# Four decoder layers on one core: the second layer's probabilities turned by a DMA, the pieces of the row maxima in one transpose

## The chip, the cores and the metric

The kernel runs on one core of a Trainium2 chip. A core has five engines that run side by side, each with its own queue of instructions: TensorE (PE, matrix products; PEld is its loading of weights), VectorE (DVE), ScalarE (ACT), GpSimd (POOL) and SyncE (SP, which issues all DMAs here). Matrix products land in PSUM, which only PE writes and only DVE and ACT read; everything else lives in SBUF (the "arena") or in DRAM. The metric is the device time of one execution in microseconds (us), the median of several runs. The profile is of one execution more.

## The reference, cut to what matters

Four decoder layers follow each other on x of shape (16, 128, 256), each with 16 heads of 16. The second layer (L1) has two attentions with quantised operands; the third and fourth have two plain attentions each.

```python
def _fq(x, delta, zp, n_bits):                      # second layer
    xi = round(x / delta) + zp
    xq = jnp.clip(xi, 0.0, 2.0 ** n_bits - 1.0)
    return (xq - zp) * delta
...
sim = jnp.einsum('bhid,bhjd->bhij', _fq(q, dq, 128.0, 8), _fq(k, dk, 128.0, 8)) * SCALE
attn = jax.nn.softmax(sim, axis=-1)
out = jnp.einsum('bhij,bhjd->bhid', _fq(attn, dw, 0.0, 8), _fq(v, dv, 128.0, 8))
...
logits = jnp.einsum('bhqd,bhkd->bhqk', qh, kh) / jnp.sqrt(depth)      # third and fourth layer
attn = jax.nn.softmax(logits + mask, axis=-1)
out = jnp.einsum('bhqk,bhkd->bhqd', attn, vh)
```

The quantised probabilities are whole numbers from 0 to 255 times a step `dw`.

## The kernel before

**Groups and the order.** The batch of 16 is cut into 8 groups of 2 (`GB = 2`, `NG = 8`). Each group runs the whole chain of layers; groups don't depend on each other. The program first makes a list of steps (`plan.step`): a step has one or more ways (an engine, a price in us that its author wrote down, the function that issues the instructions), what it reads and what it writes. `Plan.order` then lays out all steps of all groups as a list scheduler would: it takes the step that can begin first by those prices, and among steps that can begin at the same time the one with the lowest `level` plus `LEADS[group][stage]`. `LEADS` is a table of 8 x 20 numbers, so it sets which group goes first where. Memory comes from the arena by the same pass. The instructions are then issued in that order, once, in straight line: each engine works its own list in order, and waits on semaphores for the others. So an instruction that has to wait holds up all that stand behind it on its engine.

**PE has three tilings.** "full" (128 x 128, projections, feed-forward and transposes), "rows" (four matmuls of 32 rows side by side, the scores), "cols" (four of 32 columns side by side, the products of probabilities and values).

**Second layer** (`quantized_attention`, `attention`). For one batch element `j` and half `c` of its heads (8 heads), in order: the scores on PE into the one `ps` block of PSUM; the row maxima (DVE, L1099); their subtraction (DVE, L1112); the exponential (ACT, L1118); the sums and their reciprocals times 1/dw (DVE, L1124 to L1127); the division into shares, head by head, with a magic constant that rounds to whole numbers (POOL, `share`, L1133); the bound at 255 and the cast to bf16 (DVE, L1137, block `eb`). `attention` turns `eb`, queries first, into `eT`, keys first: eight PE transposes into a PSUM block `pt` (L905) and a copy to SBUF (ACT L910 or DVE L911). When both halves are there, `out_of` issues `products` (PE, L879, 16 matmuls) into `po`, and ACT scales it by `dwv` (L1143). A step of the kind occurs 8 groups x 2 attentions x 2 elements x 2 halves = 64 times, the products 32 times.

**Third and fourth layer** (`plain_attention`, `batch`). Here the scores are computed twice: once queries first, to get the row maxima of 16 heads (DVE, L1236 or L1251), and once keys first, so that the exponentials come out already turned. The maxima must be subtracted in the second form, and this is done on PE: `split` cuts each maximum into three bf16 pieces that add up to it (block `mq`, four 128-column planes, one for each of four heads of a strip of 32 rows), four PE transposes (L1271) and a copy of 128 x 512 (ACT, L1275) turn them into `mt`, and `below` adds them to the scores by four matmuls with a matrix `three` of ones in three of 32 rows (L844, 512 columns each). The fp32 products of keys and queries follow (L833). This is done 64 times. Then come the exponential (ACT, L1302), the products with values and with ones (PE, L879, fp32) and the division (DVE, L1314, L1315).

**Weights.** `weight` loads a 256 x 256 block by a DMA on SP (L634); a block that is still in the arena is not loaded again. All DMAs stand in the one queue of SP. Feed-forward and projections are `features_first` (L675) and `tokens_first` (L688), fp32.

Of the kernel before, what the change touches and what calls it, by code (L numbers as in the profile page):

```python
# [8 lines left out]
F32 = mybir.dt.float32  # L9
BF16 = mybir.dt.bfloat16  # L10
# [6 lines left out]
P = 128  # L17
# [49 lines left out]
SLOTS = {"sm": (64, 46), "row": (128, 12), "pw": (2048, 4), "ps": (8192, 1), "mq": (1024, 4)}  # L67
# [8 lines left out]
    [83, 27, 167, 130, 306, 193, 74, 226, 213, -45, 163, -53, 159, -84, 116, -64, 214, 400, 286, 283],  # L76
    [-69, -856, -114, -260, -60, 57, -165, -14, -2, -22, -386, -90, 144, -71, -260, -59, -586, -159, -213, -106],
    [49, -47, -11, 314, -162, 407, 51, 168, -361, -27, -172, 141, -4, -107, 36, 5, -54, 235, 78, 92],
    [-16, -228, 250, -173, -19, 106, 36, 203, -176, 14, 164, 2, 299, -144, 10, 309, -45, 154, 150, -1],
    [210, 166, 422, 222, 201, 790, 324, 499, 569, 334, 435, 116, 502, 205, 259, 760, 536, 716, 652, 178],  # L80
    [330, 158, 210, 147, 392, 517, 262, 488, 490, 57, 292, 77, 380, 208, 348, 38, 542, 447, 523, 1141],
    [267, 148, 130, 158, 333, 376, 220, 605, 204, -29, 43, 216, 340, 164, 196, 435, 324, 999, 754, 951],
    [288, 156, 593, 320, 407, 313, 255, 389, 233, 323, -30, 86, 440, 164, 213, 583, 372, 760, 452, 550],
# [344 lines left out]
def decoder_stack_kernel(ctx: ExitStack, tc: tile.TileContext, a: dict, out: bass.AP):  # L428
# [19 lines left out]
    G.memset(magic, MAGIC)  # L448

# [46 lines left out]
    three = const.tile([P, P], BF16, tag="three", name="three")  # L496
    mod = const.tile([P, 32], F32, tag="mod", name="mod")
# [28 lines left out]
    def prepare():  # L526
# [5 lines left out]
        def steps_of_quantization():  # L532
# [8 lines left out]
            V.tensor_tensor(dwv, d[:, :, 2], d[:, :, 3], ALU.mult)  # L541

# [6 lines left out]
        def masks():  # L549
# [4 lines left out]
            G.tensor_tensor(three, three, mod[:, 2:3].to_broadcast([P, P]), ALU.add)  # L554

            G.tensor_scalar(m1, m1, -1.0e9, 1.0, ALU.mult, ALU.mult)

        step([("POOL", 2.5, masks)], reads=[raw, dl_token], writes=[mask_token], least=110.0)
# [308 lines left out]
    def products(eTs, vz, j, po, ones=False):  # L867

        def issue():
            for c in range(2):
                for i in range(2):
                    for s in range(4):
                        if ones:
                            lhsT = ones2[:, i, :]
                        else:
                            lhsT = vz.ap()[:, j, 4 * c + s, 2 * i : 2 * i + 2, :].rearrange("p a d -> p (a d)")
                        T.matmul(  # L879
                            po.ap()[32 * s : 32 * s + 32, 2 * ones + c, :], lhsT=lhsT,  # L880
                            rhs=eTs[c].ap()[:, 2 * s + i, :], start=(i == 0), stop=(i == 1),
                        )

        return issue

    def attention(x, wo, begin, soft, out_of, vz, dtype, after):


        plan.enter(after=after, w=1, oT=1, e=2, eT=2, **({"r": 1} if dtype == F32 else {"eb": 1}))
        wo = weight(wo)  # L890
        oT = block("m", [P, 2, NT], role="oT")
        for j in range(GB):
            ps, held = begin(j)
            eTs = []
            for c in range(2):
# [3 lines left out]
                per = 4 if dtype == F32 else 8  # L899
                for q0 in range(0, 8, per):  # L900
                    pt = block("pw", [P, per, S], dtype)

                    def turn(pt=pt, e=e, q0=q0):
                        for q in range(per):
                            T.transpose(pt.ap()[:, q, :], e.ap()[:, q0 + q, :], ident if dtype == F32 else ident_b)  # L905

                    step([("PE", 0.5, turn)], reads=[e], writes=[pt], holds=[eT])
                    step(
                        [
# [287 lines left out]
    def plain_attention(x, qxT, kvT, ws, biases, mask=None, masked=None, cost=0.9, masked_T=None, key_mask=None, held=(), may_be_empty=False, there=None):  # L1197
# [29 lines left out]
        def batch(j):  # L1227
# [41 lines left out]
            def turn(pt=pt, mq=mq):  # L1269
                for f in range(4):  # L1270
                    T.transpose(pt.ap()[:, f, :], mq.ap()[:, f, :], ident_b)  # L1271
# [198 lines left out]
```

## Time and profile before

| | |
|---|---|
| median of 3 runs | 1461.03 us (1458.67 to 1462.03) |
| the profiled execution | 1458.82 us, span of its trace 1456.7 us |
| granted TensorE clock, mean over the span | 0.993 |
| projections and feed-forward on PE (L688, L675) | 484.2 + 480.9 us busy |
| transposes L905 (probabilities), L1271 (maxima) | 40.2 us in 512, 25.1 us in 256 |
| DMA queue of SP | 138224 packets, 107.40 MB, 24.5% of 16 engines' span |

The span runs from the first to the last instruction. A group of the profile is one source line, engine, operation and shape; its line gives how often it ran, the busy time in us and the mean length of one in ns, then how long the engine was idle just before such instructions and which other engine's instruction ended most of that. On PE, lengths of single matmuls overlap, so a group's busy time is not the sum over its instructions. In the answers by stage, a line begins with the stretch and its length; then come busy us and number of instructions of PE, PEld, DVE, ACT and POOL, the granted clock, the DMA engines' busy share and GB/s. In the timeline, a line has start, length, engine, line, operation, what is written and read, the shape, and how many instructions were merged. A line of DMA issues gives what is written and read, how many, the size of one and the median time from issue to landing.

### The profile page before, as it was taken

The page shows a single profiled execution, that of the slowest core. Times are in us where ns is not written, and L with a number is a line of the kernel's source. Part 1 is how long each engine was busy: PE and PEld are TensorE (multiplying, and loading weights), DVE is VectorE, ACT ScalarE, POOL GpSimd, SP SyncE. Part 2 cuts the span into 40 slices and gives each one's busy share as a digit, 9 for nine tenths or more (in the row PEclk, how much of TensorE's full clock was granted, in tenths as well). Part 3 has the DMA queues.
Part 4 walks back from the last instruction along what each step waited for, and adds up shares of the span by engine and source line. Part 5 has one row for each costly group of instructions (what it writes and reads, how often), then busy time and mean ns, then how long its engine had stood idle before and what let it go on. Part 6 is the DMA issues. An engine that isn't in the chain of part 4 may idle for free. (4 is left out here: it accounts for less than half of the span.)

```text
span 1456.7 us, 35756 instructions
## 1 busy us (share of the span) xinstructions
PE 1398.3 (96%) x14771; PEld 1141.3 (78%) x14771; DVE 1010.9 (69%) x1555; ACT 849.7 (58%) x1490; POOL 633.3 (43%) x1415
## 2 busy tenths in 40 slices
PE   8899998999899999899999999999999999999998
PEld 6677887878678888687878777777878888787777
DVE  1665788898988779767764976779478766556431
ACT  4565676766776656565554665657556454445552
POOL 2232857455777446524432542545634234243210
PEclk9999998999999999999999999999999999999999
DMA  6566513412432122112211532211210111100000
GB/s 207 138 171 192 188 48 102 117 34 67 125 90 95 44 67 70 56 52 66 84 38 45 160 101 97 85 55 56 73 45 2 42 38 66 31 31 2 2 9 23
DMA packets 138386, 109.67 MB, mean 75 GB/s; under 512 B 72288, under 2 KB 127472, under 8 KB 138096
## 3 DMA queue, kind: packets, MB, share of 16 engines
q1 hardware_dynamic: 138224, 107.40, 24.5%
q8 instruction: 116, 1.90, 0.5%
q14 instruction: 46, 0.38, 0.1%
HBM read 80.11 MB, written 27.26 MB: 74 GB/s over the span
## 5 line engine op out<-in xcount | busy, mean ns | idle before, releaser
L688 PE MATMUL pw<-arena 128*128 128x256 f32 x2048 | 484.2, 387 | 7.3 <-ACT arena L654 3.1
L675 PE MATMUL pw<-arena 128*128 128x256 f32 x2048 | 480.9, 385 | 7.8 <-ACT arena L663 2.5
L688 PEld LDWEIGHTS pw<-arena 128*128 128x128 f32 x2048 | 383.0, 192 | 68.8 <-issue 9.3
L675 PEld LDWEIGHTS pw<-arena 128*128 128x128 f32 x2048 | 379.2, 191 | 71.0 <-issue 10.0
L1133 POOL TENSOR_SCALAR arena<-arena,sm 128x128 f32<-128x128 f32 x512 | 195.9, 403 | 107.7 <-DVE sm L1127 73.4
L1314 DVE RECIPROCAL arena<-pw 128x256 f32<-128x256 f32 x64 | 112.1, 1752 | 104.0 <-PE pw L879 86.8
L734 POOL TENSOR_TENSOR arena<-arena,rows 128x512 f32<-128x512 f32 x107 | 137.7, 1289 | 89.7 <-ACT arena L721 74.0
L833 PE MATMUL ps<-arena 32*128 32x128 f32 (+2 forms) x3328 | 153.0, 309 | 2.8 <-DVE arena L1112 1.1
L1236 DVE TENSOR_REDUCE sm<-ps 128x16 f32<-128x2048 f32 x48 | 109.6, 2283 | 36.3 <-PE ps L833 33.8
L833 PEld LDWEIGHTS ps<-arena 32*128 32x128 f32 x3072 | 116.1, 186 | 20.4 <-issue 12.0
L696 DVE TENSOR_TENSOR arena<-pw,arena 128x512 f32<-128x512 f32 x88 | 60.3, 685 | 101.2 <-PE pw L688 99.7
L801 ACT ACTIVATE arena<-pw,cols_sb 128x256 f32<-128x256 f32 x184 | 78.0, 472 | 68.3 <-PE pw L675 65.5
L1261 POOL CAST mq<-sm 128x16 bf16<-128x16 f32 x58 | 15.8, 273 | 234.2 <-DVE sm L1236 114.6
L710 POOL TENSOR_SCALAR sm<-sm 128x2 f32<-128x2 f32 x88 | 20.6, 234 | 215.0 <-DVE sm L705 200.1
L721 ACT ACTIVATE arena<-arena,sm,sm 128x256 f32<-128x256 f32 x149 | 83.2, 597 | 49.3 <-POOL sm L714 48.7
L663 ACT ACTIVATE arena<-pw,cols_sb 128x256 f32<-128x256 f32 x140 | 72.7, 563 | 50.5 <-PE pw L647 47.0
L1275 ACT COPY arena<-pw 128x512 bf16<-128x512 bf16 x64 | 37.3, 582 | 84.5 <-PE pw L1271 77.6
L879 PE MATMUL pw<-arena 128*32 128x128 f32 (+1 forms) x2560 | 82.9, 265 | 3.4 <-ACT arena L910 3.0
L1099 DVE TENSOR_REDUCE sm<-ps 128x8 f32<-128x1024 f32 x64 | 77.6, 1213 | 9.8 <-PE ps L833 9.5
L1302 ACT ACTIVATE arena<-ps 128x1024 f32<-128x1024 f32 x64 | 64.1, 1025 | 33.1 <-PE ps L833 30.3
L647 PE MATMUL pw<-ident,arena 128*128 128x128 f32 x416 | 66.8, 286 | 15.1 <-DMA arena<-in_x_dram 5.1
L910 ACT COPY arena<-pw 128x1024 bf16<-128x1024 bf16 x56 | 56.3, 1011 | 41.9 <-PE pw L905 37.2
(142 smaller groups left out, 1993.8 us busy)
## 6 DMA issues: line engine op xcount, KB each, us to landing
arena<-in_L_xattn_ff_w_dram SPq DMA_DIRECT2D x38, 256.0 KB, 3.0
mha<-arena SPq DMA_DIRECT2D x16, 512.0 KB, 4.5
ca<-arena SPq DMA_DIRECT2D x16, 512.0 KB, 3.9
arena<-mha SPq DMA_DIRECT2D x16, 512.0 KB, 4.4
arena<-ca SPq DMA_DIRECT2D x16, 512.0 KB, 4.5
dqkv<-arena SPq DMA_DIRECT2D x8, 768.0 KB, 4.0
arena<-dqkv SPq DMA_DIRECT2D x16, 384.0 KB, 4.3
arena<-in_L_xattn_W_dram SPq DMA_DIRECT2D x24, 256.0 KB, 2.8
```

The lines of the kernel that those rows point to most:

```text
L663: ("ACT", 0.54, lambda c=c: A.activation(dst.ap()[:, c, :], ps.ap()[:, c, :], AF.Identity, bias=biases(c), scale=scales(c))),
L675: T.matmul(ps.ap()[:, m, :], lhsT=w.ap()[:, k, m * P : (m + 1) * P], rhs=t.ap()[:, k, :], start=(k == 0), stop=(k == 1),)
L688: T.matmul(ps.ap()[:, j, :], lhsT=lhs(k, j) if lhs else t.ap()[:, k, j * S : (j + 1) * S], rhs=w.ap()[:, k, :], start=start and j + k == 0 ...
L721: ("ACT", 0.6, lambda j=j: A.activation(xh.ap()[:, j, :], x.ap()[:, j, :], AF.Identity, bias=nb.ap()[:, j : j + 1], scale=rstd.ap()[:, j : ...
L734: ("POOL", 1.33, lambda: G.tensor_tensor(dst.ap(), src.ap(), row(name), op)),
L801: "ACT", 0.47, lambda ps=ps, h=h, m=m, bias=bias: A.activation(h.ap()[:, m, :], ps.ap()[:, m, :], func, bias=bias),
L833: T.matmul(ps.ap()[:, s, c] if i is None else ps.ap()[:, s, c, i], lhsT=left(r, c) if i is None else left(r, c, i), rhs=right(r, c), start ...
L879: T.matmul(po.ap()[32 * s : 32 * s + 32, 2 * ones + c, :], lhsT=lhsT, rhs=eTs[c].ap()[:, 2 * s + i, :], start=(i == 0), stop=(i == 1),)
L1099: step([("DVE", 1.22, lambda: V.tensor_reduce(paired(m.ap()), ps.ap()[:, :, c], AX.X, ALU.max, negate=True))], reads=[ps], writes=[m])
L1133: G.tensor_scalar(e.ap()[:, q, :], e.ap()[:, q, :], r.ap()[:, q : q + 1], MAGIC, ALU.mult, ALU.add)
L1236: V.tensor_reduce(m.ap(), ps.ap().rearrange("p s c i k -> p (s c i) k"), AX.X, ALU.max, negate=True)
L1314: step([("DVE", 1.75, lambda po=po, r=r: V.reciprocal(r.ap(), po.ap()[:, 2:4, :]))], reads=[po], writes=[r])
```

## The change

The second layer's probabilities are no longer turned on PE: one DMA per half, issued by SP, writes `eT` from `eb` transposed, arena to arena. The bound at 255 moves from DVE to ACT: instead of `min(share, 255)` ACT computes `relu(255 - share)`, that is what is missing to 255, as a bf16 whole number. The products then add a second matmul for each of the 16, with a constant block of -255 as the moving operand (`n255`), so that `po` holds the sum of (missing - 255) times values, and `dwv` takes the opposite sign. `eb` may exist twice at a time in a section.

In the plain attentions the three pieces of the four heads of a strip are put side by side in 12 of 32 columns, so `mq` is one plane of 128 columns, one transpose turns it, and the copy has 128 columns. A matrix `three_of[:, f, :]` for each of the four heads picks its three rows; the maxima are added by 16 matmuls of 128 columns, interleaved with the fp32 products of keys and queries in one function.

The table `LEADS` has other numbers throughout, so the order of all steps of all groups is another one. In the two orders PE changes its tiling 496 and 485 times, SP issues 382 and 358 plain DMAs (and 64 transposing ones), and ACT loads a function table 52 and 48 times.

```diff
-SLOTS = {"sm": (64, 46), "row": (128, 12), "pw": (2048, 4), "ps": (8192, 1), "mq": (1024, 4)}
+SLOTS = {"sm": (64, 46), "row": (128, 12), "pw": (2048, 4), "ps": (8192, 1), "mq": (256, 4)}
...
-    [83, 27, 167, 130, 306, 193, 74, 226, 213, -45, 163, -53, 159, -84, 116, -64, 214, 400, 286, 283],
+    [-63, -89, 556, 178, 277, 402, -173, 353, 503, -568, 164, 80, 171, -563, -329, -442, 89, 106, 57, -5],
...
+    top = const.tile([P, 1], F32, tag="top", name="top")
+    G.memset(top, MAGIC + 255.0)
+    n255 = const.tile([P, S], BF16, tag="n255", name="n255")
+    G.memset(n255, -255.0)
...
+            V.tensor_scalar(dwv, dwv, -1.0, None, ALU.mult)
...
+            for f in range(4):
+                t = three_of[:, f, :]
+                G.tensor_tensor(t, mod[:, 3 * f : 3 * f + 1].to_broadcast([P, P]), mod[:, 3 * f + 1 : 3 * f + 2].to_broadcast([P, P]), ALU.add)
+                G.tensor_tensor(t, t, mod[:, 3 * f + 2 : 3 * f + 3].to_broadcast([P, P]), ALU.add)
...
-    def products(eTs, vz, j, po, ones=False):
+    def products(eTs, vz, j, po, ones=False, missing=False):
...
+                    for n in range(1 if ones or not missing else 2):
+                        for s in range(4):
...
+                            T.matmul(
+                                po.ap()[32 * s : 32 * s + 32, 2 * ones + c, :], lhsT=lhsT,
+                                rhs=n255 if n else eTs[c].ap()[:, 2 * s + i, :], start=i == n == 0, stop=i == 1 and n == missing,
+                            )
...
-        plan.enter(after=after, w=1, oT=1, e=2, eT=2, **({"r": 1} if dtype == F32 else {"eb": 1}))
+        plan.enter(after=after, w=1, oT=1, e=2, eT=2, **({"r": 1} if dtype == F32 else {"eb": 2}))
...
-                    def turn(pt=pt, e=e, q0=q0):
-                        for q in range(per):
-                            T.transpose(pt.ap()[:, q, :], e.ap()[:, q0 + q, :], ident if dtype == F32 else ident_b)
...
+                step(
+                    [("SP", 1.2, lambda e=e, eT=eT: nc.sync.dma_start_transpose(out=eT.ap(), in_=e.ap().rearrange("p q k -> p (q k)")), None, 1.0)],
+                    reads=[e], writes=[eT],
+                )
...
-            step([("DVE", 0.76, lambda: V.tensor_scalar(eb.ap(), e.ap(), MAGIC + 255.0, -MAGIC, ALU.min, ALU.add))], reads=[e], writes=[eb])
+            step([("ACT", 1.05, lambda: A.activation(eb.ap(), e.ap(), AF.Relu, bias=top, scale=-1.0))], reads=[e], writes=[eb])
...
-            m, rest, mq = small(16), small(16), block("mq", [P, 4, P], BF16)
+            m, rest, mq = small(16), small(16), block("mq", [P, P], BF16)
...
-                for f in range(4):
-                    T.transpose(pt.ap()[:, f, :], mq.ap()[:, f, :], ident_b)
...
-                laid(ps, lambda s: three[strip(s), :], lambda s: mt.ap()[strip(s)], start=masked_T is None)
...
+            step([("PE", 0.1, lambda pt=pt, mq=mq: T.transpose(pt.ap(), mq.ap(), ident_b))], reads=[mq], writes=[pt], holds=[mt])
...
+                for f in range(4):
+                    c, i = divmod(f, 2)
+                    for part in (0, 1) if i else (1, 0):
+                        for s in range(4):
+                            r = strip(s)
+                            T.matmul(
+                                pT.ap()[:, s, c, i], lhsT=kz.ap()[r, c, i, tok] if part else three_of[r, f, :],
+                                rhs=qT.ap()[r, c, tok] if part else mt.ap()[r],
+                                start=masked_T is None and part == 1 - i, stop=(f == 3 or masked_T is None) and part == i,
+                            )
```

## The prediction

> **What bounds the kernel now.** I read the busy line first, then the busy times by stage, then the groups of instructions kept apart by shape, then the timeline at single steps of TensorE.
>
> ```profile
> PE 1398.3 (96%) x14771; PEld 1141.3 (78%) x14771; DVE 1010.9 (69%) x1555; ACT 849.7 (58%) x1490; POOL 633.3 (43%) x1415
> ...
> 200.00:300.00 100.00, 93.69 (x729) 76.50 (x729) 85.99 (x144) 72.75 (x138) 61.56 (x137) 0.95 0.34 91
> 300.00:400.00 100.00, 94.12 (x1075) 77.16 (x1074) 89.54 (x149) 66.67 (x128) 60.47 (x136) 0.98 0.26 80
> 400.00:500.00 100.00, 97.59 (x635) 81.16 (x637) 85.06 (x137) 66.66 (x104) 65.87 (x139) 1.00 0.27 84
> ```
>
> TensorE (PE) is busy for 1398.3 of 1456.7 us, so its idle time in the whole span is 58.4 us. From 400 us on it is above 96% in every 100 us up to the drain at the end. Only while most groups are in the second layer (200 to 400 us) it falls to 94%, where VectorE (DVE, third pair of numbers) is near 90%. So work taken from PE should come off the time almost one for one. The chain of waits says the same: nearly all of it is PE lines following each other. The busy time of other engines matters only where it makes PE wait.
>
> ```profile
> L905 PE MATMUL pw<-ident_b,arena 128*128 128x128 bf16 x512 | 40.2, 222 | 5.2 <-DVE arena L1137 2.6 <-DVE arena L1315 1.1 <-ACT arena L1058 0.9
> L1271 PE MATMUL pw<-ident_b,mq 128*128 128x128 bf16 x256 | 25.1, 220 | 2.4 <-DVE mq L1264 1.7 <-POOL mq L1264 0.7
> L910 ACT COPY arena<-pw 128x1024 bf16<-128x1024 bf16 x56 | 56.3, 1011 | 41.9 <-PE pw L905 37.2 <-issue 3.5 <-ACT arena L1058 0.7
> L1137 DVE TENSOR_SCALAR arena<-arena 128x1024 bf16<-128x1024 f32 x64 | 50.1, 784 | 13.5 <-POOL arena L1133 7.3 <-PE pw L688 1.8 <-POOL sm L714 1.1
> L1118 ACT ACTIVATE arena<-arena,sc 128x1024 f32<-128x1024 f32 x61 | 69.1, 1145 | 19.5 <-DVE arena L1112 18.7 <-POOL arena L1074 0.6
> L1275 ACT COPY arena<-pw 128x512 bf16<-128x512 bf16 x64 | 37.3, 582 | 84.5 <-PE pw L1271 77.6 <-issue 6.8
> L833 PEld LDWEIGHTS ps<-arena 32*128 32x128 f32 x3072 | 116.1, 186 | 20.4 <-issue 12.0 <-DVE sm L1236 1.6 <-DVE sm L1251 1.0
> ...
> 220.23 0.62 PE L905 MATMUL pw<-ident_b,arena 128*128 128x128 bf16 x8 [0.89 <-ACT arena L1058]
> 249.12 0.41 PE L879 MATMUL pw<-arena 128*32 128x128 bf16 x16
> 612.94 0.40 PE L844 MATMUL ps<-arena,three 32*128 32x512 bf16 x4 [0.18 <-ACT arena L1302]
> 613.15 1.04 PE L833 MATMUL ps<-arena 32*128 32x256 f32 x16
> 531.30 1.99 PE L688 MATMUL pw<-arena 128*128 128x256 f32 x8
> 533.23 0.97 PE L879 MATMUL pw<-arena 128*32 128x128 f32 x28
> 1440.56 12.25 PE L688 MATMUL pw<-arena 128*128 128x256 f32 x56
> 202.14 1.93 SPq L1029 DMA_DIRECT2D do<-arena  x4
> ...
> arena<-dqkv SPq DMA_DIRECT2D x16, 384.0 KB, 4.3
> do<-arena SPq DMA_DIRECT2D x64, 32.0 KB, 2.3
> ```
>
> A matmul's own duration (222 ns) overlaps the next one's, so a PE step is priced by how fast its instructions follow. Eight transposes take 0.62 us, the last ends 0.22 after it starts: 0.40 / 7 = 0.057 us each. Sixteen column-tiled bf16 products (four at once) take 0.41 us: (0.41 - 0.22) / 3 = 0.06 us for each set of four. Four row-tiled bf16 matmuls of 512 columns hold PE for 0.21 us (612.94 to 613.15). Full fp32 matmuls follow at 12.25 / 56 = 0.22 us; eight of them would take 1.75, and the next step, in another tiling, starts after 1.93: a change of tiling costs about 0.18 us.
>
> **PE, part by part.**
> - The turn of the probabilities (L905) goes: 64 steps of 8 x 0.057 = 0.456 us: -29.2 us.
> - One transpose of the maxima in place of four (L1271): 64 x 3 x 0.057 = -10.9 us.
> - The products of the second layer get 16 more matmuls with the constant -255: 32 steps x 4 sets x 0.06 = +7.7 us.
> - The maxima go into the transposed scores as 4 sets of 128 columns in place of one of 512: 64 x (4 x 0.06 - 0.21) = +1.9 us.
> - In that step fp32 and bf16 weights now alternate (fp32, two bf16 sets, two fp32, two bf16, one fp32). The trace has no such mix. An fp32 weight load lasts 0.186 us (L833, PEld); two bf16 sets cover 0.12 of it. Bounds: nothing, if the load is hidden as it is behind L844 today, up to four changes at half a change of tiling, 64 x 4 x 0.09 = 23 us. I take 2 x 0.03 x 64 = +4 us, nearer the lower end, as the loads run ahead in every row shown.
> - Changes of tiling: counted in the two instruction orders, 496 before and 485 after: -11 x 0.18 = -2 us.
>
> Sum on PE: -29.2 - 10.9 + 7.7 + 1.9 + 4 - 2 = -28.5 us, between -32.5 and -9.5 by the weights alone.
>
> **The other engines.** DVE loses L1137 (50.1 us) and its few copies of the turned blocks (5.4 us), most of it in the stage where it is near 90%. ScalarE (ACT) loses 56 copies of 1.01 us, gains 64 Relu over 128x1024 at about 1.1 (between L910's 1.01 and L1118's 1.15), and its copies of the turned maxima shrink from 512 to 128 columns (0.58 to about 0.3 us): -56 + 70 - 18 = -4 us. GpSimd (POOL) makes eight more constants of about 0.4 us near 110 us, long before the third layer needs them. These count nothing while PE has other work; the cover is the eight interleaved groups, and if it is gone each costs its own length once a batch.
>
> **The new wait.** The path of half a batch element's probabilities was cut to bf16 on DVE, turned on PE, copied on ACT (0.78 + 0.62 + 1.01 = 2.4 us); it becomes Relu on ACT and a DMA from arena to arena. The trace has no such transfer. Issue: at least 0.4 us on SP; at most eight times one of the four `do` transfers (1.93 / 4), 3.9 us, if the queue issues the eight 128x128 blocks one by one. Landing: at least 2.3 us (the small `do` pieces); at most 8 x 2.3 = 18.4 us, if the blocks land one after another. I take 4.3 us, the row of `arena<-dqkv`, which is nearest in size and in its short pieces. What hides it: summing PE's steps, at the prices above, over the new order from each second-layer score step to the product step of the same rank leaves a median of 30 us of other PE work (before: 22). The chain between, idle engines assumed, is 4 x 1.22 (L1099 and L1112, two halves) + 1.15 + 1.69 (sum and reciprocal, L1124 to L1127) + 3.23 (L1133, eight of 0.40) + 1.1 + 0.4 + 4.3 = 16.7 us; one of the 32 pairs has less. On SP, 64 turns stand among 358 other transfers (382 before: 24 loads of weights fewer, since more are found loaded). Each turn waits for ACT, and behind it wait weight loads, whose lateness PE would feel next. I take +2.5 us of new idle time on PE, net of what DVE's relief gives back; bounds -17 (all idle time of 100 to 400 us in the table by stage) and the late landing below.
>
> [...] No row shows the DMA's price.
>
> **Sum.** The profiled execution took 1458.82 us: a span of 1456.7 and 2.1 around it. 1458.8 - 28.5 + 2.5 = 1432.8. It lies 2.2 below the median of the three runs, 1461.03, so the median of the new runs should be 1434 to 1435: I say 1434.
>
> **Rivals.**
> 1. *The turns land late, and PE stands at the products* (slower). For it: no row shows this DMA, and the chip would move 64 x 256 KB in short pieces through one queue. Against it: `arena<-dqkv` moves more bytes in pieces of 192 bytes in 4.3 us. With 18.4 us of landing the chain is 30.8 us, 18 of the 32 pairs are short, by 148 us in all; as a stall at one pair gives the others time, I count half: 1458.8 - 28.5 + 74 = 1504. It decides from the landing at which half the shortfall is 28 us: about 12 us. [...]
> 2. *ACT becomes the place where everything queues* (no change). The Relu waits for POOL's eight instructions, and behind it on ACT stand copies out of PSUM that PE needs. For it: L1137 waited for POOL for 7.3 us on DVE, and ACT evacuates most of PE's banks. Against: it is 60 to 73% busy there. At 0.45 us for each of 64 it gives the whole gain back: 1459.
> 3. *More is won*: the relief of DVE takes away most of the 17 us of idle time between 100 and 400 us, and the mixed weights cost nothing: 1458.8 - 32.5 - 10 = 1416.
> 4. *The order, filled in anew, fits the chip worse*, with PE idle half as long again (58 + 29 us): 1459 as well, or above if the turns add to it.
>
> **How the numbers follow.** Forecast (1422 to 1448): 0.56. Rival 1 at 12 us and above, 1463 to 1504: 0.13; between 4.3 and 12 us it lies inside 1434 to 1459. Rivals 2 and 4: 0.19, spread from 1448 to 1475 around 1459. Rival 3: 0.12. A measurement of this kernel tells 0.2% (2.9 us) from no change. Faster: 0.56 + 0.12 + 0.07 of rivals 2 and 4 = 0.75; within 0.2%: 0.05; slower: 0.13 + 0.07 = 0.20. The range 1415 to 1465 leaves out most of rival 1 and the edges of rivals 3 and 4.
>
> **What would show it.** Right: PE's busy time 1366 to 1372 us and its share still above 95%; no L905 rows; the products' bf16 rows at 1024 and near 21 us; turns landing in 3 to 6 us; PE idle 50 to 70 us. Wrong: product rows (column-tiled bf16) with tens of us of idle time ended by the DMA; weight loads on SP ended by ACT's Relu; rows of ACT evacuations with PE waiting behind them; the mixed scores step much longer than 0.21 us above the old one.

## The result and the profile after

The median after is 1451.34 us (1447.18 to 1455.95, 7 runs) against 1461.03 us (7 runs of the kernel before beside them): ratio 0.9944, 95% interval 0.9927 to 0.9961. The change gains 9.7 us, where 27 us were forecast. The range and the sign held; the size did not. A second set of runs gave 1453.44 us (ratio 0.9951, 0.9939 to 0.9964).

The profiled execution took 1455.95 us, the longest of its seven, with a span of 1454.2 us. The busy line of the page of the kernel after:

```profile
PE 1383.8 (95%) x15347; PEld 1129.2 (78%) x15347; DVE 967.8 (67%) x1528; ACT 835.2 (57%) x1477; POOL 595.1 (41%) x1405
```

PE is busy 14.5 us less than before (1398.3), not 26 to 32 as forecast, and idle for 70.4 us instead of 58.4 (the span less the busy time). The same three stretches of 100 us as before (PE, PEld, DVE, ACT, POOL, clock, DMA share, GB/s):

```profile
200.00:300.00 100.00, 87.94 (x747) 70.71 (x748) 86.03 (x149) 69.31 (x113) 73.09 (x167) 0.95 0.43 98
300.00:400.00 100.00, 88.52 (x702) 73.34 (x702) 79.95 (x136) 71.58 (x120) 61.97 (x143) 0.95 0.44 111
400.00:500.00 100.00, 91.78 (x874) 74.49 (x874) 88.55 (x138) 68.54 (x119) 63.52 (x161) 0.94 0.32 78
```

Here is the new idle time: 31.8 us in these 300 us, against 14.6 before, and the granted clock fell from 0.95, 0.98 and 1.00 to 0.95, 0.95 and 0.94. Of these 17.2 us more, 11.1 lie between 380 and 420 us, where PE is busy for 25.92 us after and 37.05 before. From 500 to 1400 us PE is busier than before.

The groups of the changed steps, kept apart by shape (busy us, mean ns, idle before):

```profile
L1288 PE MATMUL ps<-arena 32*128 32x128 f32 x2048 | 97.4, 299 | 1.9 <-DVE arena L1113 0.9 <-ACT arena L1309 0.5 <-DVE sm L1238 0.4
L1288 PE MATMUL ps<-arena,three_of 32*128 32x128 bf16 x1024 | 37.4, 216 | 0.0
L892 PE MATMUL pw<-arena 128*32 128x128 bf16 x512 | 19.6, 228 | 6.7 <-DMA arena<-arena 5.7 <-ACT arena L812 1.0
L892 PE MATMUL pw<-n,arena 128*32 128x128 bf16 x512 | 19.4, 227 | 0.0
L1270 PE MATMUL pw<-ident_b,mq 128*128 128x128 bf16 x64 | 14.1, 225 | 0.1
...
L1139 ACT ACTIVATE arena<-arena,top 128x1024 bf16<-128x1024 f32 x64 | 73.3, 1147 | 32.7 <-POOL arena L1134 26.8
L1272 ACT COPY arena<-pw 128x128 bf16<-128x128 bf16 x63 | 16.4, 262 | 75.8 <-PE pw L1270 73.5 <-ACT arena L812 0.8 <-ACT arena L793 0.8
```

L905 has no row any more, L1270 has 64 transposes instead of 256, and the second products with `n255` stand beside the first. The Relu takes 1.147 us and the small copy 0.262, as forecast (about 1.1 and 0.3). The turn by DMA, from the answer on its source line (L913):

```profile
L913 SPq DMA_TRANSPOSE arena<-arena x64: 1231/1232/2709, 193.4 to 1007.5; - x64
DMA to landing us min/median/max: 3.0/3.1/5.1
```

It occupies SP for 1.232 us and lands 3.1 us (median) after its start, better than the 4.3 taken. The largest waits of PE after (us in total, times, longest):

```profile
PE ps L844 <- DVE arena L1113: 10.2, 3, 5.0
PE pw L658 <- DMA arena<-in_x_dram: 6.3, 2, 5.0
PE pw L658 <- ACT arena L732: 5.8, 2, 3.9
PE pw L892 <- DMA arena<-arena: 5.7, 3, 3.0
```

The turn costs PE 5.7 us in three waits. The largest item is another: score steps of the second layer (L844) that wait for DVE's subtraction (L1113). The same wait in the kernel before:

```profile
PE ps L833 <- DVE arena L1112: 1.1, 2, 0.6
```

With all waits of PE added up by the engine that ended them, the picture is broader: ACT ended 22.2 us before and 32.7 after, DVE 17.8 and 20.6, DMAs 7.9 and 12.7, POOL 2.5 and nothing. So most of the added waiting ends with ACT, whose waits grew longer and not more (33 before, 32 after).

Two of the three waits for L1113 stand in one place, which the timeline of the kernel after shows (PE first, then DVE; start, length):

```profile
389.57 0.40 PE L844 MATMUL ps<-arena 32*128 32x256 bf16 x8
395.01 0.62 PE L844 MATMUL ps<-arena 32*128 32x256 bf16 x8 [5.05 <-DVE arena L1113]
...
401.42 0.62 PE L844 MATMUL ps<-arena 32*128 32x256 bf16 x8 [2.93 <-DVE arena L1113]
401.96 3.78 PE L699 MATMUL pw<-arena 128*128 128x256 f32 x8
...
408.98 1.89 PE L699 MATMUL pw<-arena 128*128 128x256 f32 x8
414.73 1.11 PE L658 MATMUL pw<-ident,arena 128*128 128x128 f32 x4 [3.86 <-ACT arena L732]
...
390.02 1.23 DVE L1100 TENSOR_REDUCE sm<-ps 128x8 f32<-128x1024 f32 x1 [0.45 <-PE ps L844]
391.28 1.22 DVE L1113 TENSOR_TENSOR arena<-ps,sm 128x1024 f32<-128x1024 f32 x1
392.42 1.21 DVE L1100 TENSOR_REDUCE sm<-ps 128x8 f32<-128x1024 f32 x1
393.74 1.23 DVE L1113 TENSOR_TENSOR arena<-ps,sm 128x1024 f32<-128x1024 f32 x1
```

The order puts two score steps one behind the other on PE. There is one `ps` block, so the second waits until DVE has gone through both halves of the first: four instructions of 1.22 us, a gap of 5.05 us. The gap has an aftermath. Eight matmuls of L699 take 3.78 us at 402 us and 1.89 us at 409, exactly half. The stretches around them show why (the first figure behind the five pairs is the granted clock):

```profile
389.00:394.00 5.00, 0.96 (x11) 0.42 (x11) 4.37 (x6) 4.96 (x8) 5.00 (x15) 1.00 0.33 62
394.00:407.70 13.70, 8.07 (x91) 5.24 (x91) 13.42 (x18) 10.01 (x23) 8.85 (x27) 0.50 0.44 89
407.70:414.50 6.80, 3.17 (x15) 2.46 (x13) 6.52 (x18) 4.99 (x8) 6.34 (x19) 1.00 0.43 83
414.50:418.00 3.50, 3.27 (x32) 2.15 (x36) 2.35 (x4) 1.77 (x3) 3.42 (x8) 0.51 0.44 84
```

Right after the gap PE was granted half its clock, for 13.7 us, and once more after the next gap. Work done at half clock counts double as busy time (3.78 against 1.89 us). So I count three things for every profile: idle time; the busy time that fell into stretches of half clock, by the trace's clock records, half of which is lost; and what remains, the work at full speed. The work, half of the busy time at half clock and the idle time add up to the span. These columns are of the one profiled execution of each kernel; for after, 1, 5, 7 and 13 it was the longest of its runs.

| kernel | median us | ratio to before, 95% interval | PE busy | idle | busy at half clock | work at full speed |
|---|---|---|---|---|---|---|
| before | 1461.03 | | 1398.3 | 58.4 | 18.2 | 1389.2 |
| after | 1451.34 | 0.9944 (0.9927 to 0.9961) | 1383.8 | 70.4 | 37.2 | 1365.2 |
| after, once more | 1453.44 | 0.9951 (0.9939 to 0.9964) | 1381.2 | 72.3 | 31.8 | 1365.3 |
| 1 maxima first | 1444.02 | 0.9892 (0.9876 to 0.9908) | 1372.6 | 73.2 | 34.5 | 1355.3 |
| 2 no wait for the turn | 1452.76 | 0.9956 (0.9944 to 0.9968) | 1377.8 | 72.3 | 23.9 | 1365.8 |
| 3 bound on DVE | 1473.51 | 1.0099 (1.0081 to 1.0117) | 1386.8 | 84.7 | 39.4 | 1367.1 |
| 4 turn twice | 1546.84 | 1.0605 (1.0583 to 1.0627) | 1405.8 | 136.0 | 72.5 | 1369.6 |
| 5 maxima alone, old order | 1454.72 | 0.9962 (0.9948 to 0.9977) | 1397.1 | 59.9 | 30.2 | 1382.0 |
| 6 turn alone, old order | 1501.06 | 1.0282 (1.0263 to 1.0300) | 1390.3 | 108.9 | 60.9 | 1359.9 |
| 7 after, old table | 1513.36 | 1.0366 (1.0340 to 1.0393) | 1403.0 | 109.6 | 70.4 | 1367.8 |
| 8 before, new table | 1573.24 | 1.0777 (1.0750 to 1.0803) | 1431.0 | 139.7 | 81.0 | 1390.5 |
| 9 without -255 | 1450.09 | 0.9929 (0.9916 to 0.9941) | 1374.5 | 73.8 | 32.2 | 1358.3 |
| 10 maxima first, table refilled | 1438.56 | 0.9853 (0.9838 to 0.9868) | 1368.6 | 68.1 | 23.4 | 1356.9 |
| 12 short sum | 1444.91 | 0.9895 (0.9875 to 0.9915) | 1375.7 | 67.7 | 21.6 | 1364.9 |
| 13 short sum, before | 1453.26 | 0.9949 (0.9931 to 0.9966) | 1399.3 | 55.4 | 21.3 | 1388.7 |

The last column behaves as a count of work should: 1389.2, 1388.7 and 1390.5 for the instructions of before in three kernels of very different times, and 1364.9 to 1369.6 for all those that issue the matmuls of after. It rises by 4.4 us in 4, where PE has 65 us more idle time, so between kernels of very different idle time a difference of 4 us tells nothing; where the order is the same and the idle time alike it repeats to 1 us (after twice, 2, 12). Between the profiles of before and after, PE's work fell by 24.0 us, half of the busy time at half clock adds (37.2 - 18.2) / 2 = 9.5, and idle time adds 12.0: together -2.5, the difference of the spans. The medians differ by more (9.7) because the clock of after varies from run to run, and the profiled execution had the lowest: its seven runs go from a span of 1454.2 us at a mean clock of 0.985 to 1445.4 at 0.992. So 9.5 is the half clock of a long run. Over all runs with a clock on record the mean is 0.992 before (48 runs) and 0.988 after (12 runs). The span times the clock, which leaves the loss by half clock out, falls by 12.3 us, close to 24.0 - 12.0; the half clock then takes back about 5 us.

### The profile page after: what moved, and what is told of

It is laid out like the page before. It is cut to its first block, busy times and chain, and to the rows that moved or that the text cites. A ratio compares the mean times of both kernels' runs of the same rounds, so it can differ in the third digit from the quotient of the medians.

```text
span 1454.2 us, 36922 instructions
## 1 busy us (share of the span) xinstructions
PE 1383.8 (95%) x15347; PEld 1129.2 (78%) x15347; DVE 967.8 (67%) x1528; ACT 835.2 (57%) x1477; POOL 595.1 (41%) x1405
## 4 chain that ended last, share of the span: by engine, by line
PE 65%; DVE 4%; ACT 1%; issue 1%; DMA 0%; POOL 0%; SPq 0%; DVEq 0%; ACTq 0%
PE pw L686 22%; PE pw L699 19%; PE pw L892 9%; PE ps L1288 6%; PE ps L844 5%; PE ps L855 2%; PE pw L658 2%; DVE sm L1238 1%; DVE arena L1113 1%; DVE sm L1100 0%; DMA arena<-in_L_xattn_ffn_w_dram 0%; PE pw L1270 0%; DVE sm L1125 0%; POOL arena L1134 0%; DVE arena L1302 0%
## 5 line engine op out<-in xcount | busy, mean ns | idle before, releaser
L699 PE MATMUL pw<-arena 128*128 128x256 f32 x2048 | 481.9, 387 | 7.5 <-ACT arena L665 3.5
L699 PEld LDWEIGHTS pw<-arena 128*128 128x128 f32 x2048 | 384.0, 192 | 71.6 <-issue 8.8
L1134 POOL TENSOR_SCALAR arena<-arena,sm 128x128 f32<-128x128 f32 x512 | 186.1, 385 | 108.8 <-DVE sm L1128 43.2
L1263 POOL CAST mq<-sm 128x16 bf16<-128x16 f32 x54 | 12.7, 234 | 233.3 <-DVE sm L1238 109.3
L732 ACT ACTIVATE arena<-arena,sm,sm 128x256 f32<-128x256 f32 x143 | 79.7, 594 | 35.4 <-POOL sm L725 34.2
L1288 PE MATMUL ps<-arena 32*128 32x128 f32 x2048 | 97.4, 299 | 1.9 <-DVE arena L1113 0.9
L844 PE MATMUL ps<-arena 32*128 32x256 f32 (+1 forms) x1280 | 86.0, 376 | 10.7 <-DVE arena L1113 10.2
L892 PE MATMUL pw<-arena 128*32 128x128 f32 (+1 forms) x2560 | 88.6, 266 | 7.7 <-DMA arena<-arena 5.7
L1288 PEld LDWEIGHTS ps<-arena 32*128 32x128 f32 x2048 | 75.8, 188 | 23.7 <-issue 15.5
L1139 ACT ACTIVATE arena<-arena,top 128x1024 bf16<-128x1024 f32 x64 | 73.3, 1147 | 32.7 <-POOL arena L1134 26.8
L1100 DVE TENSOR_REDUCE sm<-ps 128x8 f32<-128x1024 f32 x64 | 77.7, 1215 | 16.0 <-PE ps L844 15.7
```

Of the source, the lines that this page charges most:

```text
L699: T.matmul(ps.ap()[:, j, :], lhsT=lhs(k, j) if lhs else t.ap()[:, k, j * S : (j + 1) * S], rhs=w.ap()[:, k, :], start=start and j + k == 0 ...
L732: ("ACT", 0.6, lambda j=j: A.activation(xh.ap()[:, j, :], x.ap()[:, j, :], AF.Identity, bias=nb.ap()[:, j : j + 1], scale=rstd.ap()[:, j : ...
L844: T.matmul(ps.ap()[:, s, c] if i is None else ps.ap()[:, s, c, i], lhsT=left(r, c) if i is None else left(r, c, i), rhs=right(r, c), start ...
L892: T.matmul(po.ap()[32 * s : 32 * s + 32, 2 * ones + c, :], lhsT=lhsT, rhs=n255 if n else eTs[c].ap()[:, 2 * s + i, :], start=i == n == 0, ...
L1134: G.tensor_scalar(e.ap()[:, q, :], e.ap()[:, q, :], r.ap()[:, q : q + 1], MAGIC, ALU.mult, ALU.add)
L1288: T.matmul(pT.ap()[:, s, c, i], lhsT=kz.ap()[r, c, i, tok] if part else three_of[r, f, :], rhs=qT.ap()[r, c, tok] if part else mt.ap()[r], ...
```

## The experiments

**1. The sixteen bf16 matmuls of the maxima ahead of the sixteen fp32 ones; same order of steps.**

```diff
-                for f in range(4):
-                    c, i = divmod(f, 2)
-                    for part in (0, 1) if i else (1, 0):
+                for part in (0, 1):
+                    for f in range(4):
+                        c, i = divmod(f, 2)
```

> The order of the steps is that of the changed kernel; only inside the third and fourth layer's second scores step all 16 bf16 matmuls of the maxima stand ahead of the 16 fp32 ones, so that PE goes from bf16 to fp32 weights once and not twice, and the step does not begin with an fp32 load. Theory A (the mix of weights was priced too low): the step's matmuls, start to start, took 93.1 us in the changed kernel (78.6 fp32 and 14.5 bf16) against 78 before; they fall to 80 to 84, and the time falls by 8 to 13 us, to 1439 to 1443. Rival B (the loss is idle time that stays whatever PE's work is): PE's work falls as much, its idle time grows by the same, and the time stays at 1449 to 1453.

1444.02 us, 7.3 under the kernel after; PE's work is 10.0 us less (1355.3 against 1365.3), 0.16 us a step. The groups by shape of this kernel:

```profile
L1288 PE MATMUL ps<-arena 32*128 32x128 f32 x2048 | 72.3, 279 | 0.0
L1288 PE MATMUL ps<-arena,three_of 32*128 32x128 bf16 x1024 | 25.9, 218 | 2.2 <-DVE arena L1113 0.9 <-ACT arena L1309 0.9 <-DVE sm L1238 0.4
```

Both rows shrink, 97.4 to 72.3 and 37.4 to 25.9. Each fp32 set stands in the trace twice (2048 records for 64 x 16 matmuls). At full clock the second record starts 112 ns after the first; in the first fp32 set behind bf16 sets it starts 165 ns after, and in a step that begins with fp32 214. In kernel 1 each step has one set of 165 in place of two, and none of 214. So the alternation of weights cost 10 us more than the sorted order. The kind of gain is theory A's; its time range (1439 to 1443) was missed by 1 us.

**2. PE waits for no turn: the products read a constant in place of `eT`.**

```diff
-                                rhs=n255 if n else eTs[c].ap()[:, 2 * s + i, :], start=i == n == 0, stop=i == 1 and n == missing,
+                                rhs=n255 if n or missing else eTs[c].ap()[:, 2 * s + i, :], start=i == n == 0, stop=i == 1 and n == missing,
```

> The order is that of the changed kernel, and the turning DMAs run; but the second layer's products read the constant block in place of the turned probabilities, so PE waits for no turn (the output is not the attention's). Theory A (the turn's latency opens few of PE's gaps: 5.7 us in 3 waits in the changed kernel's trace): the time falls by 3 to 8 us at most, to 1443 to 1449. Rival B (PE stands because turns land late, and the gaps cost the clock too): it falls by 15 us or more, to 1436 or below.

1452.76 us: nothing gained over 1451.34, and neither theory's range was met. The waits for the turn (5.7 us) are gone, and PE is idle for 72.3 us all the same. In the waits of PE in this kernel:

```profile
PE ps L844 <- DVE arena L1113: 13.3, 3, 6.3
```

PE waits longer elsewhere: 13.3 us instead of 10.2 at these score steps, the rest in other places. At 3.1 us the turn's landing is not what holds the order up.

**3. What is missing to 255 computed on DVE, without the bound at zero, at the same place in the order.**

```diff
-            step([("ACT", 1.05, lambda: A.activation(eb.ap(), e.ap(), AF.Relu, bias=top, scale=-1.0))], reads=[e], writes=[eb])
+            step([("ACT", 1.05, lambda: V.tensor_scalar(eb.ap(), e.ap(), -1.0, MAGIC + 255.0, ALU.mult, ALU.add))], reads=[e], writes=[eb])
```

> The order is that of the changed kernel; what is missing to 255 is worked out on DVE at the same place of the order, in about 0.75 us, and not on ACT in 1.15. Theory A (ACT's Relu, which waits for POOL and holds the block e, delays DVE and so the scores; 10.2 us of PE's idle time wait for DVE L1113): PE's idle time between 200 and 500 us falls from 32 us to below 25, and the time by 4 to 10 us, to 1441 to 1447. Rival B (DVE, near 90% there, is no better place): the time is the same or up to 6 us longer, 1451 to 1457.

1473.51 us, 22 us slower than after and above both ranges. Theory A missed. The stretch of the big gap in this kernel, and the waits of PE:

```profile
380.00:420.00 40.00, 21.47 (x196) 15.37 (x196) 39.00 (x58) 19.80 (x41) 26.82 (x68) 0.78 0.34 73
...
PE ps L844 <- DVE arena L1113: 15.5, 7, 8.4
```

DVE is busy for 39.0 of these 40 us and PE for 21.5. In the new order DVE has no room there for some 0.75 us more a half (an estimate, from the 0.784 us of L1137 in the kernel before), so in this order the move to ACT belongs to the gain. That ACT holds nothing up does not follow: the run takes the Relu off ACT and loads DVE at once, and the waits of PE that ACT ended stay as long (34.3 us, 32.7 in after).

**4. The turn issued twice.**

```diff
-                    [("SP", 1.2, lambda e=e, eT=eT: nc.sync.dma_start_transpose(out=eT.ap(), in_=e.ap().rearrange("p q k -> p (q k)")), None, 1.0)],
+                    [("SP", 1.2, lambda e=e, eT=eT: [nc.sync.dma_start_transpose(out=eT.ap(), in_=e.ap().rearrange("p q k -> p (q k)")) for _ in range(2)], None, 1.0)],
```

> The order is that of the changed kernel; each turn is issued twice, the second into the same block after the first, so that it lands about 3 us later and takes SP twice as long. Theory A (the turn has slack at most places): 32 products, a third of them tight, by 3 us: the time rises by 10 to 35 us, to 1461 to 1486. Rival B (the turn's landing sets PE's time in the second layer): it rises by 60 us or more.

1546.84 us, 95 us more than after, which is rival B's size. The waits of PE, then those of SP's queue:

```profile
PE pw L892 <- DMA arena<-arena: 50.4, 17, 8.2
...
SPq L913 <- DMA arena<-arena: 140.6, 70, 4.0
```

The second turn writes where the first does, so SP waits for the first to land, up to 4.0 us, with everything behind it. Three more microseconds a turn, with SP's queue held up by as much, are more than the order can bear: 17 products wait. The run doesn't part the late landing from the queue behind it. The median cover of 30 us of PE work per pair that I had counted in the order was not slack of that size. With 2, the turn at 3.1 us costs nearly nothing, and there is little room above it.

**5. The part of the maxima alone, in the order of before** (bf16 first; four sets of 128 columns and one transpose).

```diff
-                for f in range(4):
-                    T.transpose(pt.ap()[:, f, :], mq.ap()[:, f, :], ident_b)
+                T.transpose(pt.ap()[:, 0, :], mq.ap(), ident_b)
...
-                laid(ps, lambda s: three[strip(s), :], lambda s: mt.ap()[strip(s)], start=masked_T is None)
+                for f in range(4):
+                    for s in range(4):
+                        T.matmul(
+                            ps[:, s, f // 2, f % 2], lhsT=three_of[strip(s), f, :], rhs=mt.ap()[strip(s), 0, :],
+                            start=masked_T is None and f == 0, stop=False,
+                        )
```

> The kernel before, in its own order of steps to the last one, with only the maxima's part of the change: one transpose and a copy of 128 columns in place of four and 512, and four narrow sets of bf16 matmuls in place of a wide one, all ahead of the fp32 ones. PE saves 64 x 3 x 0.057 = 10.9 us and pays 64 x (4 x 0.06 - 0.21 + 0.05) = 5 us (0.05: the fp32 load that the narrow set no longer covers). Theory A (where the order stays, PE's work comes off the time one for one): 4 to 8 us less than the kernel before. Rival B (the work saved turns into idle time in any order): within 2 us of the kernel before.

1454.72 us, 4.5 us less than the 1459.24 of before beside it, as theory A has it; PE's work is 7.2 us less. I had 10.9 for the transposes less 1.9 for the narrower sets, 9.0. The profile is of its longest run (1459.18 us), where more busy time at half clock, 30.2 us against 18.2, hides the gain.

**6. The turn alone by DMA, in the order of before** (no copy; the bound stays on DVE as it was).

```diff
-                    def turn(pt=pt, e=e, q0=q0):
-                        for q in range(per):
-                            T.transpose(pt.ap()[:, q, :], e.ap()[:, q0 + q, :], ident if dtype == F32 else ident_b)
+                    def turn(eT=eT, e=e):
+                        nc.sync.dma_start_transpose(out=eT.ap(), in_=e.ap().rearrange("p q k -> p (q k)"))
```

> The kernel before, in its own order of steps, with only the turn changed: the DMA is issued where the PE transposes stood, and the copy out of PSUM is left out; the bound stays on DVE. PE loses 29 us of transposes and ACT 56 us of copies. Theory A (an order made for a turn of 0.6 + 1.0 us has products right behind it, and the DMA lands 3.1 us after its issue): PE waits some 1.5 us at most of 64 turns, up to 96 us, half of it hidden, and the time is 1460 to 1500, no gain. Rival B (the turn by DMA is worth PE's saved work in any order): 1425 to 1440.

1501.06 us, although PE's work falls by 29.3 us, near the 29.2 of the forecast (the last column of the table is good to some 4 us where idle time differs as it does here). The time lies 1 us above theory A's range. The waits of PE, then of SP's queue:

```profile
PE pw L879 <- DMA arena<-arena: 22.8, 13, 3.6
...
SPq L904 <- DVE arena L1136: 103.7, 26, 17.8
```

The old order leaves no room for 3 us of landing, and SP stands before the turns with the loads behind them. Idle time grows by 50.5 us and half-clock busy time by 42.7. In the order of before this part of the change loses 42 us.

**7 and 8. The instructions of after with the table of before, and the other way round.**

```diff
 LEADS = [
-    [-63, -89, 556, 178, 277, 402, -173, 353, 503, -568, 164, 80, 171, -563, -329, -442, 89, 106, 57, -5],
+    [83, 27, 167, 130, 306, 193, 74, 226, 213, -45, 163, -53, 159, -84, 116, -64, 214, 400, 286, 283],
...
```

> The changed kernel's code with the table LEADS of the kernel before; the scheduler fills the order from it. Theory A (the table fits one code; PE's idle time is set by how well the order was filled, not by the instructions): PE's work as in the changed kernel, its idle time at least 25 us longer, and the time 1480 to 1540. Rival B (the table matters little): 1445 to 1460.

> The code of the kernel before with the table LEADS of the changed kernel. Theory A: 1500 to 1620, with PE's idle time and its stretches of half clock in proportion. Rival B (the new table is the better one and the code is what loses): below 1455.

1513.36 and 1573.24 us (two runs each), in both cases within theory A's range. The work is that of after and of before within 3 us; nearly all of the 62 and 112 us is idle time and half clock. Neither table fits the other's instructions, and the scale on which an order matters here is tens of microseconds.

**9. The products without the -255 term, same order.**

```diff
-            step([("PE", 0.46, products(eTs, vz, j, po, missing=True), "cols")], reads=[*eTs, (vz, j), (vz, "zero")], writes=[po])
+            step([("PE", 0.46, products(eTs, vz, j, po), "cols")], reads=[*eTs, (vz, j), (vz, "zero")], writes=[po])
```

> The changed kernel with the 32 extra matmuls of each group's products (rhs of -255) left out; the output lacks the -255 term, so it isn't the attention's. Order and all else as in the changed kernel. Theory A (TensorE's own work sets the time outside its few gaps): 5 to 8 us of TensorE work fewer, time 1443 to 1448 us, TensorE's idle time within 5 us of the changed kernel's 70. Rival B (the other engines' waits set the time; work taken from TensorE turns into idle): 1449 to 1454 us, TensorE's idle time larger by what the busy time loses.

Here 512 matmuls are left out, 16 in each of the 32 product steps. PE's work is 7.0 us less (forecast: 7.7 for adding it), and the median is 3.4 less than that of the kernel after run beside it (1453.44). Idle time rises by 1.5 us only, as theory A has it, but the median lies in rival B's interval: undecided between them.

**10. Kernel 1 with the table filled once more, other values, nothing else.** Its first row:

```diff
-    [-63, -89, 556, 178, 277, 402, -173, 353, 503, -568, 164, 80, 171, -563, -329, -442, 89, 106, 57, -5],
+    [-65, -88, 415, 226, 277, 507, -298, 403, 222, -999, -120, -162, -53, -545, -591, -187, -8, 91, 62, 521],
```

> Instructions of the kernel with the sixteen bf16 matmuls first, the table of 160 shifts that fills the order filled once more with other values; nothing else. Theory A (the lost time is TensorE's gaps in the order between 200 and 500 us, and a better filling returns part of it): 1434 to 1443 us, TensorE's idle time under 65 us and its busy time in 200 to 500 us over 270. Rival B (the gaps belong to the new instructions, whatever their order): 1443 to 1450 us. Rival C (an order filled by estimated durations fits the chip no better than the one before): over 1450 us.

1438.56 us, the fastest kernel here: 22 us under before, and its interval lies under that of kernel 1. With the same work as kernel 1 within 1.6 us, it has 5.1 us less idle time and 11.1 us less busy time at half clock. But not where I expected it. Two stages of this kernel, then the same two of kernel 1:

```profile
200.00:500.00 300.00, 266.15 (x2367) 216.44 (x2367) 257.50 (x422) 211.60 (x355) 201.34 (x476) 0.96 0.40 97
500.00:800.00 300.00, 296.76 (x3454) 242.36 (x3456) 228.15 (x339) 180.21 (x294) 136.82 (x315) 1.00 0.36 98
```

```profile
200.00:500.00 300.00, 265.44 (x2338) 216.77 (x2340) 255.52 (x423) 210.85 (x353) 200.54 (x474) 0.96 0.40 96
500.00:800.00 300.00, 293.84 (x3455) 239.62 (x3452) 220.47 (x333) 179.19 (x307) 134.81 (x305) 0.99 0.33 91
```

From 200 to 500 us PE is still idle for 33.9 us (34.6 in kernel 1), and the gap of two score steps is 6.3 us long in both. Most of the idle time that went, 2.9 of 5.1 us, lies between 500 and 800 us. The half clock is no sure part of the gain, since the profile of kernel 1 is of its longest run: at the same mean clock of 0.989 the runs have spans of 1440.4 and 1442.2 us (kernel 1) and 1436.0 to 1436.7 (this kernel, three runs). Theory A is right in its time and wrong in its place, and its marks of idle time (under 65 us) and busy time (over 270) were missed.

**11. The kernel after once more.**

> The changed kernel once more, for a profiled execution nearer to the median. Theory A (its gaps between 200 and 500 us belong to the order): time 1447 to 1456 us, TensorE idle 65 to 78 us, TensorE busy 264 to 272 us in 200 to 500 us, with the same largest waits. Rival B (the profile of the changed kernel was an odd execution): TensorE busy over 278 us in that stage, idle near 60.

The median is 1453.44 us; the profiled execution, at 1455.36, is again a long one. PE's work is 1365.3 (1365.2 in the first profile), it is busy for 265.7 us from 200 to 500 us, and L844 waits for L1113 for 11.2 us. The same largest waits recur, as theory A has it: they belong to this kernel in its order and not to an odd execution.

**12 and 13. The row sum of the second layer's probabilities shortened at 64 places, after and before.**

```diff
-                    V.tensor_reduce(r.ap(), e.ap(), AX.X, ALU.add)
+                    V.tensor_reduce(r.ap(), e.ap()[:, :, 0:32], AX.X, ALU.add)
```

> The changed kernel; the row sum of the second layer's probabilities takes 32 of the 128 columns of each head (DVE reduces 256 instead of 1024 elements), so the output isn't the attention's. Some 0.9 us less on DVE at each of 64 places, the order untouched. Theory A (between 200 and 500 us DVE is the queue that TensorE waits for: 37.35 of the 40 us from 380 to 420 us, where TensorE is busy for 25.9): TensorE's idle time falls by 8 to 20 us and the stretches at half clock shrink; time 1430 to 1443 us. Rival B (TensorE's gaps there come from GpSimd, ScalarE or the turned block, which DVE's relief does not reach): 1447 to 1454 us.

> The kernel before with the same shortened row sum, in its own order: the control. Theory A (before, DVE had slack between TensorE's steps, the gaps are few): 0 to 8 us, time 1452 to 1460 us. Rival B (relief of DVE is worth as much in either order): as many us off as the run with the changed kernel.

DVE is busy for 45.4 and 44.4 us less, 0.7 us a place and not 0.9. This relief gained 8.5 us with the order of after (1453.44 to 1444.91; half-clock busy time 31.8 to 21.6, idle 72.3 to 67.7) and 8.0 us with that of before (1461.23 to 1453.26). So DVE holds PE up in either order, by about as much; these sums are not what sets the new order apart. The time of 12 lies between the ranges of its two theories, and idle time fell by 4.6 us where theory A asked for 8 to 20; for 13, rival B came true. The gap of 5.05 us stayed as it was: it is made of L1100 and L1113, which this edit doesn't touch.

## Why the prediction was wrong

**What held.** The turn on PE: -29.2 forecast, -29.3 by experiment 6; that it agrees to 0.1 us is luck, since the measure is good to some 4 us there. The -255 products: +7.7 and +7.0. The maxima with narrower sets: -9.0 and -7.2. The Relu, the smaller copy and the landing were priced within 0.05, 0.04 and 1.2 us. PE's work fell by 24.0 us against 28.5. All eight blocks of a turn, 256 KB, land in 3.1 us; plain 256 KB loads of weights land in 2.6 to 5.8 us here (medians by weight, after).

**The step that failed** is "I take +2.5 us of new idle time on PE, net of what DVE's relief gives back". Idle time rose by 12.0 us (13.9 in the second profile), and with it came a term that the sum did not have at all: PE's time at half clock, +9.5 us (+6.8) in these profiles of long runs and about 5 over all runs. Together some 17 to 21 us stand where 2.5 were taken. Over all runs the median span fell by 7.8 us where 26 were forecast; of the 18 us between, 9.5 are idle time, about 5 half clock and 4.5 work that was not saved. The bounds I gave reached only to a late turn on the upper side. The size is that of rival 4, "the order, filled in anew, fits the chip worse", at under half its 29 us of idle time and with the clock on top. That the order decides here by tens of microseconds is shown (7, 8), and that another filling of the same instructions gives 5.5 us back (10).

With it fell the premise that work taken from PE comes off the time almost one for one. Where the order was left as it was, the time fell by 4.5 us for 7.2 us of work (5), by 7.3 for 10.0 (1) and by 3.4 for 7.0 (9).

What makes the new idle time is open beyond that. It isn't the turn's landing (2), nor DVE's row sums alone (12, 13). That the double score step near 390 us is the costliest place is read from the timeline; no run removed it. ACT ended 10.5 us more of PE's waits than before, and no run parts the order from ACT's new work. The order of the old instructions was not filled once more either, so how much of the gain of 9.7 us belongs to the instructions and how much to the new filling stays open; the 24.0 us less work on PE are theirs, but for the few changes of tiling.

**The mis-sized term**: mixed weights, +4 taken within 0 to 23. Experiment 1 measured 10.0 us of work and 7.3 of time between alternating and sorted weights. I reasoned that loads run ahead "in every row shown", but the one row with fp32 behind bf16 had a set that holds PE for 0.21 us, longer than the load of 0.186; the new sets take 0.06. Nor did 0.03 us a change follow from my rows: 0.186 - 0.12 = 0.066 would have given 8.4 us. Start to start, a change to fp32 costs 0.05 us (165 against 112 ns), and a step that begins with fp32 another 0.10 (214 against 112), which the sum did not have.

**The other rivals.** Rival 1 needed a landing of about 12 us; it was 3.1, and taking PE's wait away won nothing (2). But its threshold was too high, or the queue counts for more than it allowed: two turns of 3.1 us, one behind the other, already cost 95 us (4). Rival 2, ACT, may be part of the new idle time: in the kernel after a Relu stands among the last instructions of ACT ahead of the one that PE waited for at 380.55, 414.73 and 731.85 us, in gaps of 1.75, 3.86 and 1.92 us. Its full size, 29 us, did not come, and experiment 3 can't tell, since it loaded DVE in exchange. Rival 3 expected the relief of DVE to take most of 17 us of idle time away; between 100 and 400 us idle time grew instead, from 17.1 to 28.8 us.

**The signs I named.** No L905, turns of 3 to 6 us and PE's share above 95% (95.2%) came true, idle time (50 to 70) just failed, and PE's busy time (1366 to 1372) did not hold: half clock made it 9.5 us longer than the work, beyond what it did before, and the work was 4.5 us above the forecast. The products' rows near 21 us were a figure for whole steps: from its first start to its last end a step takes 0.63 us at full clock, 20.2 us for all 32; the groups above have 19.6 + 19.4, two rows that overlap each other.

## What to carry to other kernels

Where an order is filled in anew for a change, price the new idle time as a term of its own, with a range of the size that other orders of the same work show, and not as a remainder near zero. Price a gap on PE by the half clock that may follow it as well (1.66 us of idle time were followed by a loss of 1.7 in the kernel before), and compare kernels by PE's work at full speed, which here told within 5 us what the same instructions cost in any order, and within 1 us where the idle time was alike. Where two types of weights meet in one step, try them sorted by type: here that was worth 7 us with nothing else changed.

## What the hardware showed unexpectedly

In the traces of before and after the clock falls from full to half twelve times. Eight of these stretches lasted 3.4 us, two 6.8, one 10.2 and one 13.7. In the 3.4 us ahead of each PE had been idle for 1.6 to 3.4 us in all, and a short gap was enough. The kernel before, timeline and stretch:

```profile
370.76 1.56 PE L675 MATMUL pw<-arena 128*128 128x256 f32 x4 [1.66 <-DVE arena L998]
...
371.30:374.70 3.40, 3.40 (x10) 2.65 (x9) 3.23 (x11) 2.01 (x4) 2.20 (x7) 0.50 0.63 219
```

An idle time of 1.66 us was followed by 3.4 us at a clock of 0.50 in which PE was busy throughout, a loss of 1.7 us, as much again as the gap. The length of the gap alone doesn't decide: gaps of 2.4 us at 142 us and 2.3 us at 842 us in the same trace were followed by none. No run varied a gap alone, so which gaps are followed by half clock stays open.

Within the eight stretches of 3.4 us PE was idle for at most 0.20 us; within the four longer ones for 0.53 to 5.6 us, and most in the longest: from 394.04 to 407.69 us in the kernel after, behind the gap of 5.05 us, PE was busy for 8.06 of 13.65 us.
